# Slot sums of two graph layers kept in PSUM by VectorE; biases by TensorE in bf16 parts; self messages and equal slots handled one stage later

## The chip, the cores and the metric

The kernel runs on one core of a Trainium2 chip. The metric is device time in microseconds of one execution; the time before is the median of three runs. Engines are named as in the profile: PE is TensorE's matmul (PEld its weight load), DVE is VectorE, ACT is ScalarE, POOL is GpSimd, SP is SyncE, whose queue carries the plain transfers.

## The reference

A four-layer graph network on 6250 nodes of 256 features, with 106,250 directed edges sorted by `dst`: 50,000 random ones, their 50,000 reverses, and one self edge for each node.

```python
h = relu(layernorm(x)); x = x + L0(h)   # attention, softmax over the incoming edges, 8 heads
h = relu(layernorm(x)); x = x + L1(h)   # gated graph layer (GRU)
h = relu(layernorm(x)); x = x + L2(h)   # relational layer, 8 edge types
h = relu(layernorm(x)); x = x + L3(h)   # GAT with extra self loops, batch norm over the nodes
# L1: agg = segment_sum((h @ W.T + b)[src], dst) / max(count, 1), both ways; gi = agg @ W_ih.T + b_ih
#     gh = h @ W_hh.T + b_hh; r, z = sigmoid(i + h parts); n = tanh(i_n + r * h_n); (1-z) * h + z * n
# L2: m = segment_sum((h @ weight[type])[src], dst); h @ sl_w.T + sl_b + m / max(deg, 1)
```

The kernel has a fast way for graphs of this form (every edge has its reverse, no node has more slots than planned) and a general way, entered only where a flag `todo` says that the form does not hold.

## The kernel before

Nodes are ranked by degree and laid into 49 blocks of 128 (one node for each partition). Block `i` has `CAPS[i]` slots, from 39 for block 0 to 9 for block 48, 822 in all; a slot holds one neighbour for each of the 128 nodes, and self edges have no slot. Four stages follow a build stage, each with 822 gathers (`Slots.gather`, L1144) that POOL issues: one gather fetches 128 rows of a DRAM table by a column of indices. `Slots.fill` gathers up to 8 slots (5 in `f0`) into one chunk tile; the tags' `bufs` bound how many chunks POOL may run ahead. A stage's table must be complete before the next stage gathers from it.

- `f0` (layer 0): gathers `qv` rows; DVE multiplies them by a key and later by softmax weights, both held in PSUM; PE adds the slots with an identity matrix (L1315). Its result is table `h1`, whose rows carry the normalised features and the node's own 40 neighbour ranks.
- `f1` (layer 1): `sums(i)` gathers `h1` rows, and DVE adds the slots of a chunk pairwise in SBUF (L1401, L1404, L1408). `mirror.found` (L1210) compares the gathered rows' neighbour ranks with the node's own rank into a 40 x 40 tile, which `mirror.block` (L1215) reduces; it also compares a node's own slots with each other (L1220, L1222). `products(i)` adds the self edge, scales, and forms the gates' matmuls; the bias row `ba` is made on DVE (L1420). `gates(i)` is the GRU and the next layer norm. `messages(i)` multiplies by the eight relation matrices and stores the 1 MB block into table `rel`. `selves(i)` adds the message of the self edge with eight instructions on DVE (L1494), one for each type.
- `f2` (layer 2): gathers `rel` rows by `rel_idx`; PE adds the slots with an identity matrix (L1531); then norm, the GAT product, and table `xa`.
- `f3` (layer 3): gathers `xa`, attends, and normalises over the nodes at the end.

In `f0` and `f1` the order of PE, DVE and ACT is written out by hand (`tc.manual_schedule`): `f1` is a pipeline of five generators, one block apart, blocks 48 down to 0, whose steps are taken in the order `g, p, m, p, g, s, m, g, o, s, m, p, g, s, o, g` (`s` sums, `p` products, `g` gates, `m` messages, `o` selves). In `f2` and `f3` a scheduler orders each engine. Every engine works through its own queue in order.

`mirror.judge` (up to L1250) ends `f1`: it turns the counts into `todo`.

Of the kernel before, what the change touches and what calls it, by code (L numbers as in the profile page):

```python
# [8 lines left out]
F32 = mybir.dt.float32  # L9
# [8 lines left out]
P = 128  # L18
# [42 lines left out]
SLOTS = sum(CAPS)  # L61
RW = J + 4
# [738 lines left out]
class Slots:  # L801
# [299 lines left out]
    def group(self, pool, b0, n):  # L1101
# [24 lines left out]
        share, kind = (pool.tile([P, 7], F32, name="g" + x, tag="g" + x, bufs=1)[:, :n] for x in ("share", "kind"))  # L1126
        nc.vector.tensor_tensor(share, own, rcnt, op=ALU.mult)
# [5 lines left out]
        nc.vector.tensor_tensor(ownr, ownr, share[:, :, None].to_broadcast([P, n, R]), op=ALU.mult)  # L1133
# [29 lines left out]
class Fast(Kernel):  # L1163
# [16 lines left out]
    def constants(self):  # L1180
# [9 lines left out]
        nc.vector.memset(self.eps, EPS)  # L1190
class Mirror:
# [4 lines left out]
    def __init__(self, K, S, pool):  # L1196
        self.K, self.S, self.nc, self.pool = K, S, K.nc, pool

        self.sums = pool.tile([P, 2, NB], F32, name="mirror", tag="mirror", bufs=1)
        self.rank = pool.tile([P, NB], F32, name="own_rank", tag="own_rank", bufs=1)  # L1200
        nc = self.nc
        nc.gpsimd.iota(self.rank, pattern=[[P, NB]], base=0, channel_multiplier=1,
                       allow_small_or_imprecise_dtypes=True)
        self.hits = {}

    def found(self, i, c, n, ranks):

        if i not in self.hits:
            self.hits[i] = self.pool.tile([P, J, J], BF16, name="hits", tag="hits", bufs=2)
        self.nc.vector.tensor_scalar(self.hits[i][:, c: c + n, :], ranks, self.rank[:, i: i + 1], None,  # L1210
                                     op0=ALU.is_equal)

    def block(self, i):
        nc, n = self.nc, CAPS[i]
        nc.vector.tensor_reduce(self.sums[:, 0, i: i + 1], self.hits.pop(i)[:, :n, :], axis=AX.XY, op=ALU.add)  # L1215
        own = self.pool.tile([P, J], F32, name="own_slots", tag="own_slots", bufs=2)
        nc.scalar.activation(own[:, :n], self.S.idx[:, i, :n], AF.Copy)
        same = self.pool.tile([P, J, J], BF16, name="same", tag="same", bufs=1)
# [3 lines left out]
        nc.vector.tensor_reduce(self.sums[:, 1, i: i + 1], same[:, :n, :n], axis=AX.XY, op=ALU.add)  # L1222

    def judge(self, bad, todo):

        K, S, nc, pool = self.K, self.S, self.nc, self.pool
# [16 lines left out]
        nc.vector.tensor_sub(spare, spare, self.sums[:, 1, :])  # L1243
        nc.vector.tensor_add(spare, spare, self.sums[:, 0, :])
# [3 lines left out]
        pf = K.ps([P, 2 * D], "m")[0:1, 0:1]  # L1248
# [5 lines left out]
def sparse(ctx: ExitStack, tc: tile.TileContext, K, S, qv_d, h1_d, rel_d, xa_d, rows_d, wc_d, bc_d, b_ih, w_hh,  # L1254
# [115 lines left out]
    rel_idx = K.c([P, NB, J], I32, "rel_idx")  # L1370
    with K.stage("f1", t=2, g=3, m=3), tc.tile_pool(name="f1w", bufs=1) as wp, tc.tile_pool(name="f1", bufs=2) as pool:
# [4 lines left out]
        bc = K.row(wp, bc_d.rearrange("a n -> (a n)"), 3 * D, "bc")  # L1376
        bi = K.row(wp, b_ih, 3 * D, "b_ih")
        bh = K.row(wp, b_hh, 3 * D, "b_hh")
        nc.vector.tensor_add(bi[:, : 2 * D], bi[:, : 2 * D], bh[:, : 2 * D])
        bs = K.row(wp, b_sl, D, "b_sl")  # L1380
        rel_rows = rel_d[: NP * R, :].rearrange("(n r) d -> n (r d)", r=R)
        mirror = Mirror(K, S, wp)
# [3 lines left out]
        order = list(range(NB - 1, -1, -1))  # L1386

        def sums(i):

            h = pool.tile([P, D], F32, name="hb", tag="hb", bufs=4)  # L1390
            nc.sync.dma_start(h, K.block(h1_d, i)[:, :D])
            xt = pool.tile([P, D], F32, name="xb", tag="xb", bufs=7)
            nc.sync.dma_start(xt, K.block(x1_d, i))
            total = pool.tile([P, D], F32, name="total", tag="total", bufs=3)
            state[i] = dict(h=h, xt=xt, ins=total)
            for c, n in S.chunks(i, 8):
                v = S.fill(pool, "v", 7, h1_d, i, c, n, 8, HW, S.idx)
                m = n
                while m > 2:
                    k = m // 2  # L1400
                    nc.vector.tensor_add(v[:, :k, :D], v[:, :k, :D], v[:, m - k: m, :D])  # L1401
                    m -= k
                if m == 2:
                    nc.vector.tensor_add(total if c == 0 else v[:, 0, :D], v[:, 0, :D], v[:, 1, :D])  # L1404
                elif c == 0:
                    nc.vector.tensor_copy(total, v[:, 0, :D])
                if c:
                    nc.vector.tensor_add(total, total, v[:, 0, :D])  # L1408
                mirror.found(i, c, n, v[:, :n, D:])
                yield  # L1410
            mirror.block(i)

        def products(i):

            h, ins = state[i]["h"], state[i]["ins"]

            nc.vector.scalar_tensor_tensor(ins, h, S.own[:, i: i + 1], ins, op0=ALU.mult, op1=ALU.add)
            nc.vector.tensor_scalar(ins, ins, S.rcnt[:, i: i + 1], None, op0=ALU.mult)
            ba = pool.tile([P, 3 * D], F32, name="ba", tag="ba")
            nc.vector.scalar_tensor_tensor(ba, bc, S.has[:, i: i + 1], bi, op0=ALU.mult, op1=ALU.add)  # L1420
# [9 lines left out]
            K.product(pg, ht, wh[:, :, : 2 * D], stop=False)  # L1430
            K.product(pg, it, wc[:, :, : 2 * D], start=False)
            ph = K.ps([P, D], "g")
            K.product(ph, ht, wh[:, :, 2 * D:])
# [396 lines left out]
```

## Time and profile before

| what | us |
|---|---|
| median of 3 runs (range) | 5532.34 (5525.98 to 5544.85) |
| the profiled execution, its span | 4863.2, 4861.4 |
| busy in the span: POOL, PE, DVE, ACT | 3472.2, 2937.7, 2614.6, 858.7 |
| first to last gather: `qv` of `f0` | 295.1 to 1390.7 |
| first to last gather: `h` of `f1` | 1450.3 to 2557.9 |
| first to last gather: `rel` of `f2` | 2616.8 to 3660.9 |
| first to last gather: `xa` of `f3` | 3676.9 to 4715.1 |
| mean clock granted to TensorE | 0.739 |

The profiled execution is one single execution; it is 669 us shorter than the median of the runs. A line of a group of instructions reads: line of the kernel, engine, operation, tile written and tiles read, count, then busy time in us, mean ns of one, and the idle time of that engine just ahead of them with what ended most of it. A line of a table by stage reads: stretch, its length, then busy us and count for PE, PEld, DVE, ACT and POOL, the granted TensorE clock, the share of DMA time, and GB/s.

### The profile page before, as it was taken

The page shows a single profiled execution, that of the slowest core. Times are in us where ns is not written, and L with a number is a line of the kernel's source. Part 1 is how long each engine was busy: PE and PEld are TensorE (multiplying, and loading weights), DVE is VectorE, ACT ScalarE, POOL GpSimd, SP SyncE. Part 2 cuts the span into 40 slices and gives each one's busy share as a digit, 9 for nine tenths or more (in the row PEclk, how much of TensorE's full clock was granted, in tenths as well). Part 3 has the DMA queues.
Part 4 walks back from the last instruction along what each step waited for, and adds up shares of the span by engine and source line. Part 5 has one row for each costly group of instructions (what it writes and reads, how often), then busy time and mean ns, then how long its engine had stood idle before and what let it go on. Part 6 is the DMA issues. An engine that isn't in the chain of part 4 may idle for free. (4 is left out here: it accounts for less than half of the span.)

```text
span 4861.4 us, 32406 instructions
## 1 busy us (share of the span) xinstructions
PE 2937.7 (60%) x8413; PEld 1786.4 (37%) x8413; DVE 2614.6 (54%) x5034; ACT 858.7 (18%) x1807; POOL 3472.2 (71%) x3546
## 2 busy tenths in 40 slices
PE   6834544444447788765546888877773555555560
PEld 3423433333333444333323343434442434443450
DVE  4638888888877898877763111111122434343443
ACT  3511111222223444333221000000110000000000
POOL 5447777777747777777773777777776777777767
PEclk8967667776668988877776667677776777777775
DMA  6767777778846665555552444444445444444431
GB/s 197 217 185 224 231 230 232 235 234 239 239 155 198 196 187 182 174 168 173 160 155 93 120 119 120 123 121 124 125 128 156 113 112 114 113 114 114 115 96 53
DMA packets 328275, 775.54 MB, mean 160 GB/s; under 512 B 87464, under 2 KB 172324, under 8 KB 321552
## 3 DMA queue, kind: packets, MB, share of 16 engines
q0 software_dynamic: 196864, 595.62, 43.0%
q1 hardware_dynamic: 117358, 163.66, 9.8%
q10 hardware_dynamic: 13858, 14.09, 0.9%
q8 instruction: 70, 1.15, 0.1%
q14 instruction: 125, 1.02, 0.1%
HBM read 637.90 MB, written 135.19 MB: 159 GB/s over the span
## 5 line engine op out<-in xcount | busy, mean ns | idle before, releaser
L1144 POOL DMA_INDIRECT v<-h,rec_in x822 | 857.7, 1043 | 250.6 <-issue 232.9
L1144 POOL DMA_INDIRECT v<-rel,rel_idx x822 | 794.9, 967 | 308.1 <-issue 240.4
L1144 POOL DMA_INDIRECT v<-xa,rec_in x822 | 786.8, 957 | 267.3 <-issue 244.4
L1144 POOL DMA_INDIRECT qv<-qv,rec_in x822 | 787.3, 958 | 250.4 <-issue 202.3
L1531 PE MATMUL ps_a<-v,ident 128*128 128x256 f32 x1644 | 772.9, 578 | 214.1 <-DMA v<-rel,rel_idx 197.2
L1531 PEld LDWEIGHTS ps_a<-v,ident 128*128 128x128 f32 x1644 | 351.5, 259 | 598.8 <-DMA v<-rel,rel_idx 541.3
L1589 PE MATMUL ps_a<-v,ident 128*128 128x256 f32 x1644 | 447.6, 433 | 33.3 <-DVE v L1587 33.3
L1315 PE MATMUL ps_a<-qv,ident 128*128 128x256 f32 x1644 | 456.2, 446 | 9.1 <-DVE qv L1313 9.0
L1310 PE MATMUL ps_a<-row,ident 128*128 128x256 f32 x98 | 59.3, 708 | 628.6 <-DVE row L1309 628.6
L540 PE MATMUL ps_m<-w_rel,h2t 128*128 128x512 f32 x784 | 423.7, 702 | 1.1 <-ACT h2t L533 1.1
L1315 PEld LDWEIGHTS ps_a<-qv,ident 128*128 128x128 f32 x1644 | 371.7, 230 | 108.9 <-DVE qv L1313 44.1
L1589 PEld LDWEIGHTS ps_a<-v,ident 128*128 128x128 f32 x1644 | 362.0, 223 | 118.4 <-DVE v L1587 56.4
L1571 DVE TENSOR_TENSOR s<-v,asd 128x64 f32<-128x64 f32 (+7 forms) x124 | 26.5, 213 | 610.5 <-DMA v<-xa,rec_in 599.5
L1277 DVE TENSOR_TENSOR tmp<-qv,ps_k 128x1280 f32<-128x1280 f32 (+4 forms) x183 | 247.1, 1351 | 181.7 <-ACT ps_k L1271 95.7
L1401 DVE TENSOR_TENSOR v<-v 128x512 f32<-128x512 f32 (+2 forms) x211 | 187.5, 889 | 183.2 <-DMA v<-h,rec_in 176.4
L1310 PEld LDWEIGHTS ps_a<-row,ident 128*128 128x128 f32 x98 | 24.3, 308 | 648.3 <-DVE row L1309 579.6
L1584 PE MATMUL ps_a<-xh,ident 128*128 128x256 f32 x98 | 49.2, 598 | 352.0 <-DVE xh L1582 269.5
L540 PEld LDWEIGHTS ps_m<-w_rel,h2t 128*128 128x128 f32 x784 | 178.5, 235 | 215.2 <-issue 203.6
L1545 DVE TENSOR_TENSOR tmp<-att,xa 128x512 f32<-128x512 f32 x49 | 34.0, 694 | 411.1 <-ACT xa L1543 411.1
L1534 DVE SCALAR_TENSOR_TENSOR xb<-ps_a,rcnt_in,xb 128x256 f32<-128x256 f32 x49 | 23.7, 484 | 426.7 <-PE ps_a L1531 426.5
L1278 DVE TENSOR_REDUCE s<-tmp 128x40 f32<-128x1280 f32 (+4 forms) x183 | 247.1, 1351 | 6.3
L1313 DVE TENSOR_TENSOR qv<-qv,ps_w 128x1280 f32<-128x1280 f32 (+4 forms) x183 | 235.1, 1345 | 0.0
(298 smaller groups left out, 4280.5 us busy)
## 6 DMA issues: line engine op xcount, KB each, us to landing
rel<-res SPq DMA_DIRECT2D x49, 1024.0 KB
rows<-mrow SPq DMA_DIRECT2D x49, 512.0 KB
fx<-xb SPq DMA_DIRECT2D x147, 128.0 KB
qv<-qv,rec_in POOLq DMA_INDIRECT x822, 3.8
v<-h,rec_in POOLq DMA_INDIRECT x822, 3.1
v<-rel,rel_idx POOLq DMA_INDIRECT x822, 2.8
v<-xa,rec_in POOLq DMA_INDIRECT x822, 2.8
qv<-mrow ACTq DMA_DIRECT2D x49, 256.0 KB
```

The source lines that it names most:

```text
L540: self.nc.tensor.matmul(out, xt[:, k, :], w[:, k, :], start=start and k == 0, stop=stop and k == n - 1)
L1144: self.nc.gpsimd.indirect_dma_start(out=out, out_offset=None, in_=table, in_offset=bass.IndirectOffsetOnAxis(ap=idx, axis=0))
L1277: nc.vector.tensor_mul(tmp[:, :n, :], qv[:, :n, :D], pk[:, None, :].to_broadcast([P, n, D]))
L1278: nc.vector.tensor_reduce(s[:, c: c + n, :], tmp[:, :n, :].rearrange("p j (h d) -> p j h d", h=H), axis=AX.X, op=ALU.add)
L1310: nc.tensor.matmul(pm, K.ident, row[:, 2, :], start=True, stop=False)
L1313: nc.vector.tensor_mul(v, v, w[:, c: c + n, :, None].to_broadcast([P, n, H, DH]))
L1315: nc.tensor.matmul(pm, K.ident, qv[:, j, D: 2 * D], start=False, stop=c + j == nd - 1)
L1401: nc.vector.tensor_add(v[:, :k, :D], v[:, :k, :D], v[:, m - k: m, :D])
L1531: nc.tensor.matmul(pa, K.ident, v[:, j, :], start=c + j == 0, stop=c + j == nd - 1)
L1545: nc.vector.tensor_mul(tmp, att, xa[:, None, :D].to_broadcast([P, 2, D]))
L1584: nc.tensor.matmul(pm, K.ident, xh, start=True, stop=False)
L1589: nc.tensor.matmul(pm, K.ident, v[:, j, :D], start=False, stop=c + j == nd - 1)
```

## The change

In `f1`, a PSUM tile `ps` of two halves takes the place of the SBUF tree: the first half starts as the self edge's row times `own`, the second as slot 0, and every further instruction adds two slots to the two halves. ACT scales the second half, and one instruction joins both into `ins`. The count of reverses comes from an accumulator of the comparing instruction. Biases are split into three bf16 parts each and enter the gates' and the self loop's PSUM tiles through matmuls of 3 or 6 rows; sigmoid reads PSUM directly. The self edges' messages move to `f2`, which loads the 1 MB block of `rel` again through SP's queue, and so does the comparison of a node's slots with each other. In `f2` DVE adds the slots in PSUM, two at a time, where PE added them by identity matmuls. Block 48 comes last in `f1` and not first; `judge` is written at the end of `f2`.

```diff
     def found(self, pool, i, c, n, ranks):
+        hits = pool.tile([P, 8, J], BF16, name="hits", tag="hits", bufs=2)
+        self.nc.vector.tensor_scalar(hits[:, :n, :], ranks, self.rank[:, i: i + 1], 0.0, op0=ALU.is_equal,
+                                     op1=ALU.add, accum_out=self.found_[:, i, c // 8: c // 8 + 1])
...
+    def parts(self, pool, out, vec):
+        left = vec
+        for k in range(3):
+            part = pool.tile([1, 3 * D], BF16, name="part", tag="part", bufs=3)[:, : vec.shape[1]]
+            nc.vector.tensor_copy(part, left)
+            nc.sync.dma_start(out[k: k + 1, :], part)
+            if k < 2:
+                nc.vector.tensor_sub(left, left, part)
...
-    with K.stage("f1", t=2, g=3, m=3), ...
+    with K.stage("f1", t=1, g=3, m=2, s=2), ...
+        six = wp.tile([6, 3 * D], BF16, name="six", tag="six")
+        K.parts(wp, six[0:3, :], bc)
+        K.parts(wp, six[3:6, :], bi)
...
+        nc.sync.dma_start(has_d, has)
+        for k in range(3):
+            nc.sync.dma_start(which[k: k + 1], has_d.rearrange("(a b) p -> a b p", a=1))
...
-        order = list(range(NB - 1, -1, -1))
+        order = list(range(NB - 2, -1, -1)) + [NB - 1]
         def sums(i):
+            ps = K.ps([P, 2, D], "s")
+            nc.vector.tensor_scalar(ps[:, 0, :], h, S.own[:, i: i + 1], None, op0=ALU.mult)
             for c, n in S.chunks(i, 8):
                 v = S.fill(pool, "v", 7, h1_d, i, c, n, 8, HW, S.idx)
-                m = n
-                while m > 2:
-                    k = m // 2
-                    nc.vector.tensor_add(v[:, :k, :D], v[:, :k, :D], v[:, m - k: m, :D])
-                    m -= k
...
+                k = 0
+                if c == 0:
+                    nc.vector.tensor_copy(ps[:, 1, :], v[:, 0, :D])
+                    k = 1
+                while k < n:
+                    m = min(2, n - k)
+                    nc.vector.tensor_add(ps[:, :m, :], ps[:, :m, :], v[:, k: k + m, :D])
+                    k += m
+                mirror.found(pool, i, c, n, v[:, :n, D:])
                 yield
-            mirror.block(i)
+            rest = pool.tile([P, D], F32, name="rest", tag="rest")
+            nc.scalar.activation(rest, ps[:, 1, :], AF.Copy, scale=S.rcnt[:, i: i + 1])
         def products(i):
-            nc.vector.scalar_tensor_tensor(ins, h, S.own[:, i: i + 1], ins, op0=ALU.mult, op1=ALU.add)
-            nc.vector.tensor_scalar(ins, ins, S.rcnt[:, i: i + 1], None, op0=ALU.mult)
-            nc.vector.scalar_tensor_tensor(ba, bc, S.has[:, i: i + 1], bi, op0=ALU.mult, op1=ALU.add)
+            nc.vector.scalar_tensor_tensor(ins, ps[:, 0, :], S.rcnt[:, i: i + 1], rest, op0=ALU.mult, op1=ALU.add)
...
+            nc.tensor.matmul(pg, which[:, i, :], six[:, : 2 * D], start=True, stop=False)
+            nc.tensor.matmul(pn[:, 0, :], one3, three[:, 0, :], start=True, stop=False)
+            nc.tensor.matmul(pn[:, 1, :], which[:, i, :], six[:, 2 * D:], start=True, stop=False)
         def gates(i):
-            nc.vector.tensor_add(g, x["pg"], ba[:, : 2 * D])
-            nc.vector.tensor_add(new, x["ph"], bh[:, 2 * D:])
-            nc.vector.tensor_add(ba[:, 2 * D:], ba[:, 2 * D:], x["pi"])
-            nc.scalar.activation(g, g, AF.Sigmoid)
-            nc.vector.tensor_add(xt, xt, h)
+            nc.scalar.activation(g, x["pg"], AF.Sigmoid)
+            nc.vector.tensor_mul(new, pn[:, 0, :], g[:, :D])
+            nc.vector.tensor_add(pn[:, 1, :], pn[:, 1, :], new)
...
-        def selves(i):
-            for r in range(R):
-                nc.vector.scalar_tensor_tensor(xt, res[:, r, :], S.ownr[:, i, r: r + 1], xt, ...)
...
-                for step in (g, p, m, p, g, s, m, g, o, s, m, p, g, s, o, g):
+                if k < NB:
+                    steps = g, p, m, p, g, s, m, g, s, m, p, g, s, m
+                else:
+                    steps = p, p, g, m, m, g, g, m, p, g, m
-            mirror.judge(S.bad, S.todo)
-    with K.stage("f2", t=2, m=4, a=2), ...
+    with K.stage("f2", t=2, m=2, a=4), ...
+            own = pool.tile([P, R, D], F32, name="own", tag="own", bufs=3)
+            nc.sync.dma_start(own.rearrange("p r d -> p (r d)"), K.block(rel_rows, i))
+            pa = K.ps([P, 2, D], "a")
+            nc.vector.tensor_scalar(pa[:, 0, :], own[:, 0, :], S.ownr[:, i, 0:1], None, op0=ALU.mult)
+            for r in range(1, R):
+                nc.vector.scalar_tensor_tensor(pa[:, 0, :], own[:, r, :], S.ownr[:, i, r: r + 1], pa[:, 0, :], ...)
+            mirror.same(pool, i)
             for c, n in S.chunks(i, 8):
-                v = S.fill(pool, "v", 8, rel_d, i, c, n, 8, D, rel_idx)
-                for j in range(n):
-                    nc.tensor.matmul(pa, K.ident, v[:, j, :], start=c + j == 0, stop=c + j == nd - 1)
+                v = S.fill(pool, "v", 10, rel_d, i, c, n, 8, D, rel_idx)
+                k = 0
+                if c == 0:
+                    nc.vector.tensor_copy(pa[:, 1, :], v[:, 0, :])
+                    k = 1
+                while k < n:
+                    m = min(2, n - k)
+                    nc.vector.tensor_add(pa[:, :m, :], pa[:, :m, :], v[:, k: k + m, :])
+                    k += m
...
+            nc.scalar.activation(rest, pa[:, 1, :], AF.Copy)
-            nc.vector.scalar_tensor_tensor(xt, pa, S.rcnt[:, i: i + 1], xt, op0=ALU.mult, op1=ALU.add)
+            nc.vector.tensor_add(rest, pa[:, 0, :], rest)
+            nc.vector.scalar_tensor_tensor(xt, rest, S.rcnt[:, i: i + 1], xt, op0=ALU.mult, op1=ALU.add)
...
+        mirror.judge(wp, S.bad, S.todo)
```

## The prediction, made before the changed kernel ran

> **What bounds the kernel now.** First the table by stage, cut at the first and last gather of each stage.
>
> ```profile
> 295.00:1392.00 1097.00, 485.76 (x1654) 374.38 (x1654) 899.23 (x1246) 208.63 (x493) 832.15 (x870) 0.70 0.79 232
> 1450.00:2559.00 1109.00, 756.74 (x1976) 390.97 (x1976) 870.26 (x1874) 368.81 (x609) 858.35 (x840) 0.81 0.58 178
> 2559.00:2617.00 58.00, 33.63 (x84) 16.31 (x84) 39.62 (x89) 17.34 (x27) 0.18 (x1) 0.79 0.17 66
> 2617.00:3662.00 1045.00, 831.41 (x1922) 422.60 (x1922) 155.59 (x383) 88.91 (x237) 794.76 (x822) 0.70 0.42 122
> 3662.00:3677.00 15.00, 6.53 (x18) 3.60 (x16) 4.62 (x11) 3.94 (x9) 0.13 (x1) 0.61 0.10 36
> 3677.00:4716.00 1039.00, 548.23 (x1864) 423.03 (x1864) 401.91 (x767) 33.97 (x93) 786.68 (x822) 0.73 0.43 120
> ```
>
> `f2` and `f3` do very different work on PE and DVE and last the same. What they share is 822 gathers on POOL. The groups of instructions say why:
>
> ```profile
> L1144 POOL DMA_INDIRECT v<-h,rec_in x822 | 857.7, 1043 | 250.6 <-issue 232.9
> L1144 POOL DMA_INDIRECT v<-rel,rel_idx x822 | 794.9, 967 | 308.1 <-issue 240.4
> L1144 POOL DMA_INDIRECT v<-xa,rec_in x822 | 786.8, 957 | 267.3 <-issue 244.4
> L1144 POOL DMA_INDIRECT qv<-qv,rec_in x822 | 787.3, 958 | 250.4 <-issue 202.3
> ```
>
> A gather keeps POOL busy for 957 ns and is followed by a gap of 305 ns (the median), in which POOL waits for nothing shown: 822 x 1.262 = 1037 us. That is all of `f3` (1039). So POOL paces every stage, and each stage's time is its gathers plus what stretches or holds one. `f1` is the exception with 1043 ns. In the trace, 288 of its gathers exceed 1000 ns, and their excess over 957 is 71.4 us; in `f0`, `f2` and `f3` it is 1.5, 9.3 and 1.1. Who does it is seen in the timeline:
>
> ```profile
> 2551.31 0.96 POOL L1144 DMA_INDIRECT v<-h,rec_in  x1 [0.30 <-issue]
> 2551.73 1.95 DVE L1401 TENSOR_TENSOR v<-v 128x1024 f32<-128x1024 f32 x2 [5.02 <-DMA v<-h,rec_in]
> 2552.57 1.21 POOL L1144 DMA_INDIRECT v<-h,rec_in  x1 [0.30 <-issue]
> ```
>
> The second gather starts while DVE adds two SBUF tiles, and ends at 2553.78, 0.1 us after DVE's pair (2553.68). The long gathers of `f1` overlap L1494 most often (194 times), then L1401 (153), L1453, L1420, L1404: all with two tensor inputs in SBUF. `f0` keeps DVE busier per us (899 of 1097), but its large multiplies read one operand from PSUM, and its excess is 1.5 us.
>
> The second cost is what lies between stages. The waits of POOL:
>
> ```profile
> POOL v L1144 <- DVE todo L1250: 58.0, 1, 58.0
> ```
>
> From the last gather of `f1` (end 2558.8) to the first of `f2` (2616.8), POOL waits for the end of the pipeline and of `judge`.
>
> **The change, part by part.** (1) Stretched gathers of `f1`. Tree adds, `selves`, `ba`, the self edge's term, the compare of equal slots and most gate operations lose their second SBUF input or leave the stage; of the repeated ones none has two. I take the excess down to about 1.5, that of `f0`: -70 us. A rule speaks against this. The Trainium skill, SBUF — State Buffer, section Who interferes with whom, says that a VectorE instruction with two SBUF inputs contends only with GpSimd's reads, and infers that descriptor generation needs the write interface, which such an instruction leaves free; only 2-port modes (plain copies, `tensor_scalar`) would starve the gathers. By that rule only the compares L1210 (51 overlaps) and L1418 (15) count, 66 of 288 gathers, about 16 us. The rows disagree: L1494 and L1401 top the list, and both take two tensors, for which the page knows no such mode. I follow the rows; 16 stays as the low end.
>
> (2) The pace in `f1` otherwise. DVE loses, per block: 8 x 0.487 (`selves`), 1.01 (`ba`), 0.69, 0.42 and 0.41 (bias adds), 0.42 (`b_sl`), 0.40, and the reduces 0.83 and 0.47 with their compare 0.48: about 9 us of 17.8 (870/49). It gains a start 0.42, an accumulating compare (0.39 before; bounded by 0.8) and two small gate adds. The slot adds remain: 350 adds of 512 elements at 0.685 (row of `g<-ps_g,ba`, one PSUM input), 73 of 256 at 0.42, 49 copies at 0.41, 291 us against 269 before. DVE falls to about 600 us, PE gains four short matmuls per block (0.40 + 3 x 0.28 by the bias rows of the build stage): 757 + 61 = 818 of 1040. Neither sets the pace. Cover: seven chunks. A chunk's buffer is free 30.5 us ahead of its next gather at the least (block 45), 37 or more later. The prologue of six and three bias parts goes through SP in turn, behind 3.8 MB of weights: store, wait, store. Ahead of DVE's first sums stand those copies, and behind SP's waiting stores the first `hb` and `xb` loads. PE's first product ended 30 us into the stage; I put it 10 to 20 later, inside the 30 of cover. Were the cover used up, each us more would stop POOL; 0 to +15, taken 0.
>
> (3) The end of `f1`. Before, PE waited until 2572.0 (13 us after the last gather) for the 39-slot sum of block 0, then ran three blocks of messages and one of products until the last `rel` store at 2608.8; 8 us more covered its landing, `selves` (4.3) and `judge` (3). After, the last block has 9 slots, so PE starts on block 0 while those are gathered (11.4 us), some 20 us earlier, but then has one more round of products (5.8) and messages (9.6) plus biases: about 17. Net -3, and -2 for `judge` and `selves`, whose place the landing of 1 MB takes: -5 (-12 to +2). The 18 memsets of POOL (0.7 us) stay ahead of the first gather.
>
> (4) `f2` in its pace. PE's 1644 identity matmuls go (772.9 us busy, none of it on POOL's path): 0. DVE's load becomes 156 + self messages 49 x (0.41 + 7 x 0.487) = 187 + adds 291 + equal slots 47 + joining add 21 = 702 of 1045. In the order of instructions each block's norm chain is interleaved with the adds of the next, so POOL's ten chunks (some 100 us ahead) do not run dry. The 49 loads of 1 MB go on SP's queue, three blocks ahead; 51 MB in 1045 us is 49 GB/s beside 122, where `f0` moved 232: 0. But three operations per block now have two SBUF inputs anew: the compare (23.7 us in all) and the final scale-and-add, whose input was PSUM (49 x 0.484 = 23.7). Before, 49 x (0.69 + 0.42) = 54 us of such work gave 9.3 us of excess, so 47 more gives +8; ends 0 and +47 (every one fully in POOL's way).
>
> (5) From `f2` to `f3`, 15 us before. After the last gather come an add, an ACT copy and the joining add, 1.5 us, and `judge`'s tail, up to 2. DVE's own backlog adds to it: a block of 9 slots costs DVE 11.2 us and POOL 11.4, one of 12 costs 12.3 against 15.1, so with 1 to 2 us per block of waits on ACT and PE the last three blocks leave 3 to 6. +9 (+2 to +25).
>
> Sum against the profiled execution: -70 - 5 + 8 + 9 = -58 us, 4863.2 to 4805. The median of the runs is 669 us above the profiled execution, and no view shows where. Carried over as it is, 5474; in proportion (x 1.138), 5466. I take **5470 us**, 1.1% less. About 0.3% (17 us) can be told from no change.
>
> **Rivals.** *Gathers stretched by something else* (0.10). Then by the rule of part 1 only 16 us go: -16 - 5 + 8 + 9 = -4, 5528, no change. For it: two-port compares and scales do lie in the list. Against: L1494 and L1401 lead it.
>
> *`f2` becomes DVE's* (0.12), the slower end. DVE takes over the sums and self messages; each block averages 702/49 = 14.3 us of work against POOL's 21.3. Waits of DVE on `rest`, the square root, ReLU and the transposed product come on top, since it works in order. They decide from 8.6 us per block: 49 x (14.3 + 8.6) = 1122, which is 1045 plus the 75 us that `f1` and its end give back. At 10 us `f2` lasts 49 x 24.3 = 1191 and the time is 5532 - 75 + 146 = 5603. Against: those answers amount to some 4 us per block even uncovered, and adds of the next block lie between.
>
> *PE bounds the runs* (0.13). If the 669 us come from a lower TensorE clock than the profile's, PE would set `f1` and `f2`: at 0.45, `f2` takes 831 x 0.70/0.45 = 1293, `f1` 757 x 0.81/0.45 = 1363, together 500 us more than in the profile. Then removing PE's sums gives about 1293 - 1053 = 240 in `f2`, the biases cost 61 x 0.81/0.45 = 110 in `f1`: 5532 - 240 + 110 = 5400. For it: the unexplained time. Against: it needs under 0.56 in `f2`, and the profile granted 0.70.
>
> **How the numbers follow.** The main case has 0.65, with 5440 to 5490 as its own range. Faster: 0.65 + 0.13 = 0.78, less a little for the main case with all costs at their high ends (-58 + 39 + 15, within 0.3%): 0.77. Same: 0.10 + 0.01, slower 0.12. The range reaches to the PE rival below and the unchanged one above: 5395 to 5530.
>
> **What would show it.** Right: `h` gathers near 960 ns, `f1` near 1040 from first to last; `rel` gathers near 977; gaps near 53 and 24; DVE about 600 in `f1`, 700 in `f2`, PE far below 200 there. Wrong: `h` gathers still over 1020 (part 1); gaps of POOL on `v` buffers inside `f1` in its first 200 us (part 2) or late in `f2` (parts 4, 5); a gap to `f3` over 40 us; or a median whose distance to its profile is no longer near 669.

## The result

The changed kernel took 5620.5 us (median of 4 runs, 5609.1 to 5623.8), the kernel before 5529.9 (4 runs, 5526.0 to 5544.9): 1.015 times as long, 95% interval 1.0127 to 1.0174. The forecast was 5470, faster.

The kernel before, unchanged, was met at two levels, 5490 to 5560 us and 4857 to 4864 (medians of sets of runs), each set wholly at one of them. The profile that the prediction was made from (4863.2) lies at the lower level, the runs above at the upper one. At the lower level the changed kernel took 4804.2 against 4864.1, 0.9879 times as long (0.9862 to 0.9895). The change is 1.2% faster there and 1.5% slower here. The five sets of the experiments ran on chips 13, 11, 12, 11 and 9: the upper level on 13 and 12, the lower on 11 and 9. No chip was met at both levels, and that of the runs above is not on record, so whether the level goes with the chip can't be told.

The profile of the changed kernel is one of its own timed runs (5622.4 us, span 5620.6). Its table by stage, cut at first and last gather (stretch, its length, busy time of PE, weight loads, DVE, ACT and POOL with instructions, granted clock, share of DMA, GB/s):

```profile
334.70:1583.50 1248.80, 555.05 (x1676) 403.31 (x1677) 907.02 (x1251) 209.48 (x497) 831.31 (x869) 0.67 0.69 204
1639.20:3000.70 1361.50, 825.07 (x2082) 378.68 (x2083) 552.49 (x1297) 358.19 (x586) 788.28 (x822) 0.78 0.46 142
3000.70:3082.90 82.20, 64.69 (x174) 29.97 (x172) 35.83 (x92) 30.48 (x53) 0.71 (x19) 0.93 0.20 79
3082.90:4253.90 1171.00, 121.51 (x264) 64.31 (x264) 588.40 (x1295) 108.65 (x308) 799.54 (x822) 0.50 0.47 150
4253.90:4306.70 52.80, 13.93 (x32) 7.40 (x32) 42.68 (x118) 11.92 (x33) 0.00 (x0) 0.50 0.18 61
4306.70:5475.50 1168.80, 558.57 (x1864) 429.48 (x1864) 402.85 (x767) 35.23 (x94) 786.63 (x822) 0.70 0.38 107
```

The first and the last row are code that the change leaves alone, and both are some 130 to 150 us longer than in the profile of before (1097 and 1039). So the two profiles can't simply be subtracted. The groups of POOL in the changed kernel (busy time, mean ns of one, idle before):

```profile
L1144 POOL DMA_INDIRECT v<-h,rec_in x822 | 788.3, 959 | 573.7 <-DVE hits L1223 327.3
L1144 POOL DMA_INDIRECT v<-xa,rec_in x822 | 786.6, 957 | 434.9 <-issue 281.3
L1144 POOL DMA_INDIRECT qv<-qv,rec_in x822 | 786.5, 957 | 403.5 <-issue 367.0
L1144 POOL DMA_INDIRECT v<-rel,rel_idx x822 | 799.6, 973 | 375.6 <-issue 238.9
```

The gathers of `f1` fell from 1043 to 959 ns, as part 1 had it. But behind them stands a wait that the prediction's profile did not have: POOL stops for `hits`, the last reader of a buffer of gathered rows. The second line is the same kind of wait in `f2`.

```profile
POOL v L1144 <- DVE hits L1223: 327.3, 41, 21.1
...
POOL v L1144 <- DVE ps_a L1572: 85.7, 14, 14.6
```

### The profile page after: what moved, and what is told of

Its sections match the earlier page's. It is cut to its first block, busy times and chain, and to the rows that moved or that the text cites. A ratio compares the mean times of both kernels' runs of the same rounds, so it can differ in the third digit from the quotient of the medians.

```text
span 5620.6 us, 30604 instructions
## 1 busy us (share of the span) xinstructions
PE 2413.0 (43%) x6965; PEld 1465.6 (26%) x6966; DVE 2765.9 (49%) x5470; ACT 891.1 (16%) x1906; POOL 3406.2 (61%) x3546
## 5 line engine op out<-in xcount | busy, mean ns | idle before, releaser
L1144 POOL DMA_INDIRECT v<-h,rec_in x822 | 788.3, 959 | 573.7 <-DVE hits L1223 327.3
L1328 PE MATMUL ps_a<-qv,ident 128*128 128x256 f32 x1644 | 521.6, 475 | 211.2 <-issue 191.8
L1635 PE MATMUL ps_a<-v,ident 128*128 128x256 f32 x1644 | 471.1, 440 | 156.3 <-issue 150.0
L532 PE MATMUL ps_t<-ident,h 128*128 128x128 f32 x196 | 52.5, 361 | 1063.2 <-issue 508.8
L1635 PEld LDWEIGHTS ps_a<-v,ident 128*128 128x128 f32 x1644 | 370.6, 226 | 248.6 <-issue 165.2
L1572 DVE TENSOR_TENSOR ps_a<-ps_a,v 128x512 f32<-128x512 f32 (+1 forms) x423 | 273.5, 649 | 212.9 <-remote 91.5
L532 PEld LDWEIGHTS ps_t<-ident,h 128*128 128x128 f32 x196 | 27.9, 172 | 1103.2 <-issue 618.1
L1443 DVE TENSOR_TENSOR ps_s<-ps_s,v 128x512 f32<-128x512 f32 (+1 forms) x423 | 275.1, 650 | 12.0 <-issue 0.2
L1633 DVE TENSOR_TENSOR v<-v,ps_w 128x2048 f32<-128x2048 f32 (+7 forms) x124 | 233.0, 1914 | 0.0
L1561 DVE SCALAR_TENSOR_TENSOR ps_a<-own,ownr,ps_a 128x256 f32<-128x256 f32 x343 | 164.7, 482 | 87.5 <-DVE ps_a L1572 31.0
```

The lines of the kernel that those rows point to most:

```text
L532: nc.tensor.transpose(pt[:, k, :], x[:, k * P: (k + 1) * P], self.ident)
L1144: self.nc.gpsimd.indirect_dma_start(out=out, out_offset=None, in_=table, in_offset=bass.IndirectOffsetOnAxis(ap=idx, axis=0))
L1328: nc.tensor.matmul(pm, K.ident, qv[:, j, D: 2 * D], start=False, stop=c + j == nd - 1)
L1443: nc.vector.tensor_add(ps[:, :m, :], ps[:, :m, :], v[:, k: k + m, :D])
L1561: nc.vector.scalar_tensor_tensor(pa[:, 0, :], own[:, r, :], S.ownr[:, i, r: r + 1], pa[:, 0, :], op0=ALU.mult, op1=ALU.add)
L1572: nc.vector.tensor_add(pa[:, :m, :], pa[:, :m, :], v[:, k: k + m, :])
```

## Experiments

A ratio is to the kernel before in the same set of runs. "Upper" and "lower" are the two levels; "stalls" are the sums, counted in the trace, by which the interval from one gather's start to the next exceeds 1.262 us where it is over 2.6 us. An "answer" is the start of an instruction that waits for another engine's result. In the views, `remote` is a release for which the profile names no instruction, and `issue` a start for which it shows no release.

### First set (before: 5560 us): where is the loss?

`before_again`: no edit.

> The kernel before, unchanged, to see a profile of it that took as long as its timed runs. Both theories need that profile: the code that the change leaves alone (first and last stage of gathers) took 1096 and 1038 us from first to last gather in the one profile of before, and 1248 and 1168 in that of after. Theory A (each engine is starved from time to time in the timed executions, and the change has less cover for it in layers 1 and 2): the first and last stage again about 1248 and 1168, layer 1 about 1270 and layer 2 about 1170, so that layer 1 is shorter here than in after (1360) by nearly the whole difference of 91 us. Theory B (layer 2 became DVE's, as my slower rival had it): layer 2 about 1100 here against 1170, layer 1 about the same as in after.

It took 5562.5, its profile 5532.1. This is the profile that the prediction lacked. The same table, from `f1` on, and POOL's longest wait for DVE inside a stage:

```profile
1635.50:2920.00 1284.50, 758.87 (x1932) 386.23 (x1933) 846.22 (x1828) 358.68 (x595) 856.46 (x840) 0.76 0.50 153
2920.00:3000.70 80.70, 49.89 (x130) 24.71 (x128) 63.23 (x136) 25.58 (x41) 0.04 (x1) 0.83 0.16 63
3000.70:4186.30 1185.60, 530.64 (x1867) 402.95 (x1868) 146.80 (x360) 83.87 (x224) 792.02 (x822) 0.68 0.37 107
4186.30:4216.00 29.70, 18.45 (x72) 13.80 (x71) 13.22 (x35) 8.57 (x22) 0.00 (x0) 0.82 0.16 54
4216.00:5387.50 1171.50, 559.58 (x1864) 430.50 (x1864) 403.10 (x767) 33.85 (x93) 786.95 (x822) 0.70 0.39 106
...
POOL v L1144 <- DVE hits L1210: 165.2, 23, 15.5
```

Against it the loss of 88.5 us between the spans has a place: `f1` +77.1 (1284.4 to 1361.5), `f2` -14.6, the gap from `f1` to `f2` +1.5, that from `f2` to `f3` +23.0, the rest +1.5. POOL's wait for `hits` is there in the kernel before, too, and the change doubles it (165.2 to 327.3). And the 669 us between the prediction's profile and the runs have one too: 36 before the first gather, 152 in `f0`, 176 in `f1`, 141 in `f2`, 132 in `f3`, the rest in the gaps. They are spread over every stage, as stalls: 2.2 us in `f3` and none elsewhere in the lower profile, 166, 177, 139 and 134 us here. Theory A is met, B is not.

`f1_only`: the changed `f1`, with the self edges' messages and equal slots kept in it, and the old `f2`.

> The change in layer 1 alone: sums in PSUM, biases by PE, accumulated reverses; the self edges' messages and the equal slots stay in layer 1 and layer 2 is that of before. Theory A (layer 1 has less cover): nearly all of the loss, 5590 to 5620. Theory B (layer 2 is what costs): 5530 less the 70 us of stretched gathers, 5460 to 5500.

```diff
 to the changed kernel
+            mirror.same(pool, i)
             rest = pool.tile([P, D], F32, name="rest", tag="rest")
...
-            nc.sync.dma_start(K.block(x2_d, i), x["xt"])
...
+        def selves(i):
+            xt, res = state[i]["xt"], state[i]["res"]
...
-                v = S.fill(pool, "v", 10, rel_d, i, c, n, 8, D, rel_idx)
...
+                v = S.fill(pool, "v", 8, rel_d, i, c, n, 8, D, rel_idx)
+                for j in range(n):
+                    nc.tensor.matmul(pa, K.ident, v[:, j, :], start=c + j == 0, stop=c + j == nd - 1)
```

Measured 1.013 (1.0109 to 1.0151), 5627.7 us; `f1` 1347.1 us. Theory A is met: nearly all of the loss is there, though its 5590 to 5620 were written for a kernel before of 5530 us and not 5560.

`f2_only`: the old `f1` without `selves` and equal slots, and the changed `f2`.

> The change in layer 2 alone: slots summed in PSUM by DVE, self edges' messages and equal slots there, layer 1 as before without these two. Theory A: near before or a little slower by the longer way from layer 2 to layer 3 (52.7 against 15 us), 5530 to 5575. Theory B: 5600 and more.

```diff
 to the kernel before
-                for step in (g, p, m, p, g, s, m, g, o, s, m, p, g, s, o, g):
+                for step in (g, p, m, p, g, s, m, g, s, m, p, g, s, g):
...
-            mirror.judge(S.bad, S.todo)
...
+            own = pool.tile([P, R, D], F32, name="own", tag="own", bufs=3)
...
+            mirror.same(pool, i)
...
-                v = S.fill(pool, "v", 8, rel_d, i, c, n, 8, D, rel_idx)
...
+                v = S.fill(pool, "v", 10, rel_d, i, c, n, 8, D, rel_idx)
...
+                    nc.vector.tensor_add(pa[:, :m, :], pa[:, :m, :], v[:, k: k + m, :])
...
+        mirror.judge(wp, S.bad, S.todo)
```

Measured 0.9981 (0.9971 to 0.9992), 5548.7 us: `f2` -13.7, the gap behind it +23.3 us. So the loss is layer 1's. Its `f1`, which does less on DVE (655 us busy against 846) and whose gathers are shorter (1018 ns), is not faster for it: 1291.6 against 1284.4 us.

`f1_sums`: of the change only the sums of `f1` in PSUM.

> Of the change only the sums of layer 1 in PSUM with the self edge's term (and one buffer of PSUM less for the transposed tiles and for the messages); biases, order of blocks, reverses, self edges and layer 2 as before. If the sums and the buffers of PSUM cost the time: as slow as the change of layer 1 alone. If biases, order or reverses do: about 5480, since the stretched gathers are fewer (half of them overlapped the additions that are replaced).

```diff
 to the kernel before
-    with K.stage("f1", t=2, g=3, m=3), ...
+    with K.stage("f1", t=1, g=3, m=2, s=2), ...
...
-                    nc.vector.tensor_add(v[:, :k, :D], v[:, :k, :D], v[:, m - k: m, :D])
...
+                    nc.vector.tensor_add(ps[:, :m, :], ps[:, :m, :], v[:, k: k + m, :D])
...
+            nc.scalar.activation(rest, ps[:, 1, :], AF.Copy, scale=S.rcnt[:, i: i + 1])
```

Measured 1.0105 (1.0081 to 1.0128). `f1` is 52.6 us longer than in `before_again`: the gathers give back (1041 to 985 ns), but stalls rise from 177 to 273 us. These sums are two thirds of the loss in `f1`; the biases, the accumulator and the order of blocks add little (`f1_only` is 10 us longer in `f1`).

Where the time goes inside is best seen at PE's products of messages, in front of which PE never stands in the prediction's profile. Their group in `f1`, first of that profile, then of `before_again`, of `f1_sums` and of the changed kernel (idle before them and its releasers at the end):

```profile
L540 PE MATMUL ps_m<-w_rel,h2t 128*128 128x512 f32 x736 | 399.1, 705 | 0.0
```

```profile
L540 PE MATMUL ps_m<-w_rel,h2t 128*128 128x512 f32 x720 | 408.9, 731 | 55.4 <-ACT res L1481 32.8 <-issue 17.8 <-ACT h2t L533 4.8
```

```profile
L540 PE MATMUL ps_m<-w_rel,h2t 128*128 128x512 f32 x720 | 420.5, 742 | 126.5 <-issue 96.1 <-ACT res L1481 30.3
```

```profile
L541 PE MATMUL ps_m<-w_rel,h2t 128*128 128x512 f32 x710 | 412.9, 737 | 317.5 <-issue 202.6 <-ACT res L1515 114.8
```

In the changed kernel PE stands 317 us in front of work of 413 us. The timeline of the changed kernel shows one case:

```profile
2118.01 6.11 PE L541 MATMUL ps_m<-w_rel,h2t 128*128 128x512 f32 x8
...
2136.31 0.60 ACT L1515 ACTIVATE res<-ps_m 128x512 f32<-128x512 f32 x1 [10.33 <-remote]
...
2146.11 0.60 ACT L1515 ACTIVATE res<-ps_m 128x512 f32<-128x512 f32 x1 [9.20 <-remote]
...
2148.35 0.16 DVE L1500 RECIPROCAL rs<-rs 128x1 f32<-128x1 f32 x1 [16.88 <-ACT rs L1498]
...
2163.51 0.95 POOL L1144 DMA_INDIRECT v<-h,rec_in  x1 [21.14 <-DVE hits L1223]
```

PE's eight products, two results that fill both banks of the messages, are recorded as done at 2124.1. ACT, idle since 2126.0, starts its copy of the first result at 2136.3, and that of the second at 2146.1, though PE has run nothing in between but one more result's products. The square root stands behind these copies, DVE waits 16.9 us for it, and behind that stand two more waits of DVE and its next sums (2159.2 to 2163.2). With these a buffer of rows comes free, and POOL, which has stood for 21.1 us, goes on. In the lower profile such an answer comes at once. Between the end of PE's two transposes of `h2` and ACT's copy of them lie 0.09 us on average in the prediction's profile (47 copies of `f1`, none over 1 us) and 5.9 us in `before_again` (45 copies, 18 over 1 us, the longest 40.9).

### Second set (before: 4859 us): buffers and order

`before_psum`, `after_t2` and `after_m3` deal out the banks of PSUM in `f1` otherwise, `after_order` moves one step.

```diff
 before_psum
-    with K.stage("f1", t=2, g=3, m=3), ...
+    with K.stage("f1", t=1, g=3, m=2), ...
 after_t2, after_m3 (the second and third line)
-    with K.stage("f1", t=1, g=3, m=2, s=2), ...
+    with K.stage("f1", t=2, g=2, m=2, s=2), ...
+    with K.stage("f1", t=1, g=2, m=3, s=2), ...
 after_order
-                    steps = g, p, m, p, g, s, m, g, s, m, p, g, s, m
+                    steps = g, p, m, p, g, s, g, m, s, m, p, g, s, m
```

> The kernel before with only the buffers in PSUM that the change leaves to layer 1: one instead of two for the transposed tiles, two instead of three for the messages; two banks lie idle, the arithmetic is that of before. Theory A (fewer buffers in PSUM chain PE, ACT and DVE together, so that each late answer stops the next engine): layer 1 as long as with the sums in PSUM, 1330 to 1345 us from first to last gather, and 5580 to 5600. Theory B (the sums on DVE themselves, or their order, are what costs): layer 1 about 1285 and 5530 to 5545 as before.

> The changed kernel with the banks of PSUM in layer 1 dealt out anew: two buffers for the transposed tiles, two for gates, two for messages, two for sums (1, 3, 2, 2 in the change, where the gates need two a block). Theory A: DVE's waits on ACT's copy of the transposed tiles (128.7 us in layer 1) mostly go, and 20 to 60 us of the time with them: 5560 to 5600. Theory B: 5610 to 5625, as changed.

> The changed kernel with one buffer for the transposed tiles, two for gates, three for messages, two for sums. Theory A: PE waits less for ACT's copies of messages (114.8 us in layer 1), ACT reaches the square root earlier, DVE's wait on it (207.3 us) shrinks: 5570 to 5610, but less gain than the second buffer for the transposed tiles if that is the tighter of the two. Theory B: 5610 to 5625.

> The changed kernel with one step of layer 1 moved in the written order: the gates' step that ends in ACT's square root goes ahead of the first two products of messages and ACT's copies of them, and nothing else. Theory A, and the largest single wait of DVE in layer 1 is as the waits name it (207.3 us for the square root, which stands behind those copies on ACT): that wait goes below 80 us, and if DVE's waits are what holds the buffers of gathered rows, 5540 to 5590. If the wait only moves to the next answer (the tanh that DVE then asks for earlier): 5605 to 5630.

The expectations were written for the upper level, and this set fell on the lower: they could not be decided here. Instead: `before_psum` 1.0003 (0.9994 to 1.0011), `after_t2` and `after_m3` both 0.9875 (0.9858 to 0.9891), 4797.6 and 4798.0 us, `f1` 1037.5 and 1037.9 with 0 and 1.4 us of stalls; `after_order` 0.9999 (0.9990 to 1.0007).

`after_order` shows that at the lower level, too, a written order can use up the cover, the chunks that POOL runs ahead. The square root, moved ahead of ACT's copies of messages, now stops these until DVE has got there, and PE waits for their banks. PE's products in `f1`, DVE's two longest waits there, and POOL's longest on an engine:

```profile
L541 PE MATMUL ps_m<-w_rel,h2t 128*128 128x512 f32 x727 | 433.3, 752 | 157.4 <-ACT res L1515 157.4
```

```profile
DVE new L1484 <- PE ps_g L541: 239.8, 42, 7.2
DVE xb L1523 <- PE ps_m L541: 168.9, 40, 7.0
...
POOL v L1144 <- DVE hits L1223: 56.7, 18, 10.4
```

At this level there is no wait on the square root to win: it is 0.5 us in the unmoved kernel (`after_c` below). The two waits on PE, together 409 us here, are 73.1 and 2.9 us there. `f1` got 51 us of stalls (1091.1 us against 1038.0), which ate the change's whole gain. What the moved step does at the upper level was not run.

### Third set (before: 5490 us): the same at the upper level

> The changed kernel, unchanged. The kernel before has now been measured at two levels: 5530 to 5560 us where the changed one took 5620, and 4859 where the changed one has not been measured. Theory C (the sum of the prediction holds where answers between engines come at once, and its carrying over of 669 us was the mistake): where before takes about 4860, 4795 to 4810, layer 1 near 1038 us from first to last gather; where before takes about 5550, 5610 to 5630 with layer 1 near 1360. Theory D (the buffers in PSUM cost even where answers come at once): where before takes 4860, 4830 or more with stalls in layer 1.

> The changed kernel with two buffers for transposed tiles and two for gates in layer 1. It took 4797.6 where before takes 4859 (layer 1: 1037.5). Where before takes about 5550: by theory A (fewer buffers chain the engines) 5560 to 5600; if the buffers do not matter there, 5610 to 5625.

> The kernel before with the fewer buffers in PSUM that the change leaves to layer 1. It took 4860.6 where before takes 4859, so the buffers cost nothing there. Where before takes about 5550: by theory A 5580 to 5600 with layer 1 at 1330 to 1345; if the buffers do not matter, as before.

> Of the change only the sums of layer 1 in PSUM. Where before takes about 4860: fewer stretched gathers (985 ns on average against 1043 in the kernel before), so layer 1 shorter by 40 to 50 us and 4810 to 4820. Where before takes about 5550: 5585 to 5625 as measured.

The edits are those of the kernels of the same names above. `after_again` 1.016 (1.0129 to 1.019), 5587.1 us, the same loss once more; its `f1` is 60.7 us longer than in `before_psum_b`. `before_psum_b` 1.0002 (0.9986 to 1.0018): in the kernel before, fewer buffers in PSUM for the transposed tiles and the messages cost nothing, so the account by these buffers (theory A) falls. `after_t2_b` 1.0205 (1.0181 to 1.0228): a second buffer for transposed tiles, taken from the gates, doesn't help, it is slower than the change. DVE stands as long as before in front of the instruction that waited for ACT's copy of those tiles (L1489: 119 us, 120 in `after_again`), only the name of the releaser is another; in front of the one that follows the square root it stands 275 us as against 212, and `f1` had 319 us of stalls as against 292. `f1_sums_b` 1.0086 (1.006 to 1.0113), `f1` 51.8 us longer than in `before_psum_b`, with the same banks for the other tiles: so the sums do it, and not the banks that they take from others. About half of the 52 us is DVE's own work (849 to 875 us busy), the other half its waits (419 to 446 us idle). The tile of the sums itself has two buffers (`s=2`) where `total` had three; that was not varied.

### Fourth and fifth set (before: 4864 and 4857 us): the changed kernel itself, and one hop

The sums bring one hop from DVE to ACT and back (`rest`). `before_hop` adds such a hop to before, `f1_sums_rest` and `after_rest` take it out.

```diff
 before_hop
             mirror.block(i)
+            hop = pool.tile([P, D], F32, name="hop", tag="hop")
+            nc.scalar.activation(hop, total, AF.Copy)
+            state[i]["ins"] = hop
 f1_sums_rest (to f1_sums), after_rest (to the changed kernel)
-            nc.scalar.activation(rest, ps[:, 1, :], AF.Copy, scale=S.rcnt[:, i: i + 1])
+            nc.vector.tensor_scalar(rest, ps[:, 1, :], S.rcnt[:, i: i + 1], None, op0=ALU.mult)
```

> The kernel before with one hop more in layer 1: after a block's sums ACT copies the total into another tile, and DVE goes on from the copy, as the change does with the part of its sum that it calls rest. Theory H (the hop from DVE to ACT and back, by which ACT waits for the block's last gathered rows before it goes on, is what makes layer 1 longer where answers come late): where before takes about 5500, 1.005 to 1.01 times before, and layer 1 longer by 25 to 55 us; where before takes about 4860, nothing (layer 1 at 1108, 4855 to 4865). Theory N (the many additions of two slots are what does it): as before in both.

> The sums of layer 1 in PSUM alone, with the rest scaled by DVE and not by ACT. It was 1.0105 and 1.0086 times before with ACT. Theory H: 0.998 to 1.003 where before takes about 5500. Theory N: 1.007 to 1.011. Where before takes about 4860: 4805 to 4820 by either.

> The changed kernel with the rest scaled by DVE and not by ACT in layer 1. Theory H: of the 77 us that layer 1 lost where answers come late, 40 to 60 come back: 1.003 to 1.009 times before instead of 1.016. Theory N: 1.014 to 1.018. Where before takes about 4860: 4795 to 4810 by either.

> The changed kernel unchanged, beside the others. Where before takes about 4860: 4795 to 4810 with layer 1 near 1038, by the prediction's sum. Where before takes about 5500: 1.015 to 1.018 times before, as twice measured.

> The kernel before with one hop from DVE to ACT and back after a block's sums in layer 1. It was 0.9998 times before where before takes 4864. Where before takes about 5500: theory H (that hop is what makes layer 1 longer there) 1.005 to 1.01, layer 1 longer by 25 to 55 us; theory N (the additions of two slots are) as before within 0.2%.

> The sums of layer 1 in PSUM alone, the rest scaled by DVE. It was 0.9926 times before where before takes 4864. Where before takes about 5500, where the same with ACT was 1.0086 and 1.0105: theory H 0.998 to 1.003, theory N 1.007 to 1.011.

Both sets fell on the lower level. `after_c`, the changed kernel without an edit, took 4804.2, 0.9879, as theory C had it for this level; theory D, by which the buffers cost here too, falls. Its table by stage, from `f1` on:

```profile
1452.50:2490.50 1038.00, 789.93 (x2131) 372.64 (x2132) 569.65 (x1341) 365.42 (x603) 788.06 (x822) 0.88 0.62 188
2490.50:2546.70 56.20, 44.33 (x124) 20.48 (x122) 15.53 (x48) 21.18 (x37) 0.75 (x20) 1.00 0.25 95
2546.70:3598.70 1052.00, 132.57 (x288) 70.07 (x288) 602.31 (x1393) 118.41 (x333) 802.01 (x822) 0.50 0.54 170
3598.70:3614.20 15.50, 2.88 (x8) 1.54 (x8) 6.47 (x19) 2.75 (x8) 0.04 (x2) 0.50 0.11 35
3614.20:4652.40 1038.20, 545.97 (x1864) 421.50 (x1864) 402.18 (x767) 35.29 (x94) 786.21 (x822) 0.73 0.44 120
```

and its products of messages, in front of which PE now never stands, and DVE's longest wait in `f1`, which is for rows not gathered yet:

```profile
L541 PE MATMUL ps_m<-w_rel,h2t 128*128 128x512 f32 x729 | 372.0, 670 | 0.0
...
DVE ps_s L1443 <- DMA v<-h,rec_in: 302.8, 200, 5.9
```

The others: `after_rest` 0.9883 (0.9866 to 0.9899), no different from the change; `before_hop` 0.9998 (0.9990 to 1.0007) and, in the fifth set, 1.0000 (0.9991 to 1.0009); `f1_sums_rest` 0.9926 (0.9909 to 0.9943), 4826.4 us and so just above the 4805 to 4820 expected, and 0.9931 (0.9914 to 0.9948). At this level the hop costs nothing. Whether it, or the many additions of two slots, is what makes the sums slow at the upper level was to be told there, and no set fell on it again: by experiment it stays open. The traces of the upper level speak against the hop. These are all of ACT's waits for `rest` in `f1` of `f1_sums_b` that are over 1 us:

```profile
ACT rest L1411 <- DVE hits L1210: 25.9, 1, 25.9
ACT rest L1411 <- DVE ps_s L1405: 3.9, 1, 3.9
```

Both lie in the first 35 us of the stage, and DVE never stands in front of `ins`, which needs `rest`; the stalls of that stage come to 252 us. So ACT hardly waits there for a block's last rows, and theory H needs that wait.

`f1_sums_rest` says something else. Its `f1` is 35.7 us shorter than that of `before_hop` beside it, with gathers of 994 ns against 1044. So the sums alone are about half of part 1, and the other operations with two SBUF inputs the rest: `f1_only`, which keeps the self messages and equal slots, lies at 971 ns, the whole change at 959.

## Why the prediction was wrong

**The step that failed** is the last of the sum: "The median of the runs is 669 us above the profiled execution, and no view shows where. Carried over as it is, 5474". I took a difference that I could not place for a constant to which gains add. It is no constant: the changed kernel's own distance between the levels is 5620.6 - 4797.7 = 823 us by the spans of its profiles, that of the kernel before 5532.1 - 4861.4 = 671. The 152 us that it has more lie in `f1` (323.5 against 175.9, +148), in the gap behind `f2` (+22) and, the other way, in `f2` (119 against 141, -22). At the upper level POOL stalls in every stage, and the change made these stalls more in `f1` (25 to 41) and fewer in `f2` (32 to 17). Why answers are late at that level stays open. I had listed the distance to the median as something that would make me wrong, but the only rival that I built on it was a lower clock of PE.

**The sum itself** was right for the execution it was made from. At the lower level, before (profile, span 4861.4) against `after_c` (span 4797.7): `f1` -70.5 us (forecast -70 for part 1, 0 for part 2), gap to `f2` -1.9 (-5), `f2` +7.0 (+8), gap to `f3` +0.5 (+9), and +1.2 in code that the change leaves alone. Together -63.7 by the spans and -59.9 by the medians, forecast -58. The total is better than its parts: parts 3 and 5 were off by +3 and -8.5 us, and part of that cancels.

**Part 1** holds at both levels: 959 ns. At the upper level, too, what of `f1` is not stalls fell by 67.3 us (1107.5 to 1040.2). The Trainium skill (SBUF — State Buffer, Who interferes with whom) infers that two SBUF inputs leave descriptor generation alone; by that only 16 us would have gone. For these gathers the inference does not hold: instructions with two inputs in SBUF were taken away, and the stretching went with them. It is the second input, and not the result in SBUF: in `f1` of `after_c`, 47 gathers lie beside `xb<-ps_g,xb` (L1492), which reads PSUM and SBUF and writes SBUF, and none of them is over 1000 ns. By what path the input does it is not shown. I was right to follow the rows. My list of overlaps left out L1210, which has one tensor input and lies beside 51 long gathers; counted again, the top is L1494 (214), L1401 (159), L1404 (72), then L1210.

**Part 2** ("0 to +15, taken 0") failed at the upper level alone, and it is the term of the sum that was mis-sized there. The cover of seven chunks was measured where no answer is late. There it is never used (DVE waits for rows, above). At the upper level `f1` is no longer paced by POOL alone, and stalls rose by 144 us, 177 to 321, against the 67 us that part 1 gave. DVE's busy time fell somewhat below the forecast (570 at the lower level, 552 here, forecast 600) and bought nothing, because DVE then stands longer (810 us idle in `f1` as against 442 in `before_again`), most of it in front of instructions that wait for ACT or PE: 207 us for the square root, 129 behind ACT's copy of the transposed tiles.

```profile
DVE rs L1500 <- ACT rs L1498: 207.3, 18, 17.2
DVE ps_g L1489 <- ACT hit L1461: 128.7, 17, 10.8
```

**Parts 3, 4 and 5.** Part 3 is within its bounds at both levels (-1.9 and +1.5). Part 4, +8, was +7.0, with `rel` gathers of 976 ns; at the upper level -14.6: the stalls of `f2` fell from 139 to 117 us. Part 5, +9 (2 to 25), was +0.5, below its range, and +23.0: the backlog of DVE that I feared (42.7 us busy in the gap, 6.5 at the lower level) is there only where answers are late.

**The rivals.** *Gathers stretched by something else* is refuted by 959 ns. *`f2` becomes DVE's* ends on the right side by luck, with the wrong mechanism: `f2` alone was 0.9981, and the stage got shorter. *PE bounds the runs* had the right question, what differs between profile and runs, and the wrong answer: taking PE's sums out of `f2` gave 14.6 us and not 240, and the granted clock of `f2` in the slower profile of before was 0.68, not under 0.56. What remains of it is that answers to PE's work are late there, at nearly the same clock.

No version beat both kernels at both levels. At the upper one `f2_only` is 0.2% better than before; at the lower one `after_t2` and the change are equal within their intervals. `f2_only` was not run at the lower level.

## What to carry to other kernels

When the profiled execution and the timed runs lie 14% apart, no sum made on the profile may be carried to the runs by adding a constant: get a profile as long as the runs first, and compare the stages that the change leaves alone. A wait that is covered in one execution is covered only as long as every answer in the chain behind it comes at once; with late answers an in-order engine that had less of its own work to do just waited longer, and unloading DVE (846 to 552 us busy in `f1`) was worth nothing. And a step moved ahead in one engine's written order stands in the way of what it overtook: ask who waits for that (`after_order` lost its whole 1.2% so).

## What the hardware showed beyond this

The two levels themselves, 4860 and about 5500 us for the same program with nearly the same granted clock (0.74 and 0.71 over the span), on different chips as far as is recorded. At the upper level there are stretches in which an engine's instructions come one at a time, at steps of about 0.7 us. PE in the last stage of `before_again`, on products that wait for nothing shown, with a weight load recorded between each two (4823.19, 4825.29):

```profile
4821.79 0.58 PE L1589 MATMUL ps_a<-v,ident 128*128 128x256 f32 x1 [2.47 <-DMA v<-xa,rec_in]
...
4824.58 0.58 PE L1589 MATMUL ps_a<-v,ident 128*128 128x256 f32 x1 [2.22 <-issue]
...
4825.99 0.59 PE L1589 MATMUL ps_a<-v,ident 128*128 128x256 f32 x1 [0.82 <-issue]
...
4827.94 0.95 POOL L1144 DMA_INDIRECT v<-xa,rec_in  x1 [6.24 <-PE ps_a L1589]
```

POOL then stops, 6.2 us here, some 27 times in that stage. In the changed `f2`, where PE has little to do, DVE goes at such steps instead (4097.51, 4098.90, 4099.60, 4100.31 in `after_again`). In the kernel before, the loads of instructions are as many at both levels (209 transfers, 0.62 us each at the lower, 0.61 at the upper), and the packets of the gathers take nearly the same time (43.0% of 4861 us, 38.4% of 5532), so neither is the difference. The traces of the upper level hold a quarter of the semaphore updates that those of the lower one hold (20,611 against 77,284 for the kernel before, 19,601 against 78,150 for the changed one), and those kept come thicker just after POOL has stopped. Whether what thins the records also holds the engines, or both have a third cause, these runs don't show.
